# 3x3 stage, first two groups: the additions of an item's columns recorded in front of the next combinations

## The chip, the cores and the metric

The kernel runs on one core of one Trainium2 chip. Its time is the device time of that core in microseconds, the median of three runs. All arithmetic is in 32-bit floating point.

## The reference

Two residual bottleneck layers follow one another on an image tensor of 64 x 1024 x 14 x 14:

```
def layer(x, w1, b1, g1, be1, w2, b2, g2, be2, w3, b3, g3, be3, residual_scale):
    out = relu(bn(conv(x, w1, b1, stride=1, pad=0), g1, be1))     # 1x1, 1024 -> 256
    out = relu(bn(conv(out, w2, b2, stride=1, pad=1), g2, be2))   # 3x3,  256 -> 256
    out = bn(conv(out, w3, b3, stride=1, pad=0), g3, be3)         # 1x1,  256 -> 1024
    out = softplus(residual_scale)[0] * out
    return relu(x + out)
# bn: mean and variance over batch and pixels, per channel, of the batch itself
```

The case concerns the 3x3 convolution of both layers. Its input and output have 256 channels, held as two slots of 128 partitions.

## The kernel before, in words

Each layer is a 1x1 stage, then the 3x3 stage (`conv2`), then a 1x1 stage. The 256-channel image `y_all` stays on chip throughout. In the 3x3 stage it is worked on in place.

**Tiling.** The 64 images are cut into 8 groups of 8 images (`NG`, `GI`). The rows of a group are not convolved directly: combinations of rows are formed, each is multiplied by transformed filters, and the products are combined back into output rows. There are six such combinations per group (`NF`), taken in the pairs (1, 2), (3, 4), (5, 0). In this text they are **items**, numbered through a layer from 0 to 47. Items 0 to 5 belong to group 0, items 6 to 11 to group 1. Items of the pair (3, 4) have three tile rows, and their matmuls are 168 columns wide; the others have four and are 224 wide.

**Making an item's input.** `combine(g, pair)` records on VectorE (DVE) the work for both items of a pair. For the pair (3, 4) its first part is one large difference of rows into the scratch tile `steps` (L768), two combinations into `r` (L771 and L772, through the helper at L636), and `add_columns`, the additions into `sums` (L667). Its second part, recorded one step later, is `diffs` (L689) and `v` (L681). Each part ends with the loads of filters (`ua`, `ub`) for one item, issued on the SP queue. In what follows "the combinations of item 8" means the first part for the pair of items 8 and 9, and likewise "of item 14" for items 14 and 15.

**Multiplying.** TensorE (PE) takes, for each item in turn, four sets of eight matmuls: `l` of this item, the even `columns` of this item, `m` of the next item, and the odd `columns` of this item. `m` is copied by ScalarE (ACT) into the banks `columns` of the next item (L846, or L844 with a bias for the first item of a group) before that item's `columns` matmuls accumulate on it. There are **two** pairs of banks `columns`, so item i+2 gets the banks of item i. `l` is copied by ACT into `ls` (L866).

**Finishing.** `finish()` is a generator that takes one item per step. Each step begins with `add_to` (L885), which adds the banks `columns` and `ls` into a tile `f`: the additions of columns. This is the last reader of the item's banks. Further DVE work then combines the `f` tiles into output rows of `y`. For groups 0 and 1 the last step of a group, items 5 and 11, first records `middle_rows()` (four `stt` on DVE at L636, `y<-f,fb` and `y<-fc,fa`), then the `add_to`, then two accumulating DMAs on the POOL queue (L982). For later groups `middle_rows()` comes at an earlier step.

**Order.** A planner turns the recorded program into one instruction stream for each engine. Work recorded earlier has precedence, but an instruction that is not yet ready by the planner's reckoning is passed by a later one that is; instructions marked `keep_in_program_order` stay behind everything recorded before them on their engine. TensorE's matmuls are so marked. The DVE instructions that the change touches are not.

The loop over items records, for item k, its `l` copies, its even columns, the start of the next item, ACT's side work (`long_work`), its odd columns, `finished.send(item)`, and the part of the combinations for an item three places on. For k = 5 and k = 11 alone (`NF - 1`, `2 * NF - 1`) that last part is recorded ahead of `finished.send`.

Of the kernel before, what the change touches and what calls it, by code (L numbers as in the profile page):

```python
# [69 lines left out]
RT, NF = 4, 6  # L70
# [20 lines left out]
def bottlenecks(ctx: ExitStack, tc: tile.TileContext, x, w1s, w2s, w3s, pars, out):  # L91
# [85 lines left out]
    def busy(psum, tag, n, with_=None):  # L177

        v = ident if with_ is None else with_
        for i in range(n):  # L180
            matmul(psum.tile(448, tag), v, v[:, :1].to_broadcast([P, 448]), start=True, stop=True)
# [412 lines left out]
    def conv2(b, par, aff, early, rest):  # L594
# [434 lines left out]
        def items():  # L1029
            for g, pair in pairs[1:]:  # L1030
                yield from combine(g, pair)

        def long_work(g, k):

            i = ("norm 0", "norm 1", 0, 1, 2, 3)[k] if g else (None, "norm 0", "norm 1", None, None, None)[k]
            if g + 1 == NG:
                i = (0, 1, 2, 3, None, None)[k]
            if i in ("norm 0", "norm 1"):  # L1040
                s = int(i[-1])
                norm(s, y_grp[:, s, g + 1], aff, act)
            elif i is not None:
                o = i // 2
                moment(y_all[:, o, (g - 1) * GPX : g * GPX], idle, o, i % 2, g - 1)
# [13 lines left out]
        coming, finished = items(), finish()  # L1059
# [28 lines left out]
        queue = queue[1:] + list(itertools.islice(coming, 1))  # L1088
        for k in range(1, NG * NF):
            item, more = queue[0], queue[1:2]  # L1090
            qs = both_columns
            copy = act if k < 4 else nc.scalar.activation
            if k > 1:
                item.middle(copy=copy)
            if more:
                item.columns(qs[0])
                qs = qs[1:]
            for v in more:
                v.start(copy)
            if k == 1:  # L1100
                queue += list(itertools.islice(coming, 1))
            long_work(*divmod(k, NF))
            item.columns(*qs)
            if k in (NF - 1, 2 * NF - 1):
                queue += list(itertools.islice(coming, 1))
            finished.send(item)
            queue = queue[1:] + list(itertools.islice(coming, k not in (1, NF - 1, 2 * NF - 1)))
        busy(psum, "m", 7)

    def conv3(psum, t, o, w3, tag=None):  # L1110
# [405 lines left out]
    class Border:  # L1516
# [17 lines left out]
        def begin(self):  # L1534


            self.xpool.close()
            self.scope = ExitStack()
            early = self.scope.enter_context(
                tc.tile_pool(name=f"early_{self.b}", bufs=1, side="right", reuse_waits="tile")  # L1540
            )
            self.work = conv2(self.b, par[self.b], self.aff, early, self.rest)
# [193 lines left out]
```

## Time and profile before

| what | value |
|---|---|
| median of three runs | 1921.81 us (1921.47 to 1922.11) |
| the profiled execution | 1921.13 us, of which the span of the profile is 1919.3 us |
| granted TensorE clock | 1.0 |
| busy share of the span: PE, DVE, ACT, POOL | 99%, 80%, 57%, 30% |
| 3x3 stage of the first layer | about 304 to 584 us |
| 3x3 stage of the second layer | about 1258 to 1540 us |
| in 304 to 584 us: PE, DVE, ACT, POOL busy | 277.0, 269.3, 198.2, 45.6 us of 280 |

Starts are in microseconds from the beginning of the span. In the timelines each row is a run of like instructions: start, duration, engine, line, operation, output<-input, number, and in square brackets the idle time before it with what ended it. The recorded durations of neighbouring DVE instructions overlap by some 0.08 us, so the distance between starts is the time that one of them takes from its engine. In the list of stretches the columns are: stretch, its length, then the busy time and the number of instructions for PE, PEld (weight loads), DVE, ACT and POOL, the granted clock, the share of the DMA engines and GB/s. In the chain of waits each row is a piece of the chain that ended last: start, duration, engine, tile and line.

### The profile page before, as it was taken

To read this page: it belongs to the slowest core of one execution; us is meant where nothing else is said; L and a number is where in the kernel's file an instruction comes from. 1 tells how busy PE (TensorE), PEld (TensorE's weight loads), DVE (VectorE), ACT (ScalarE), POOL (GpSimd) and SP (SyncE) were. 2 spreads that over 40 slices of the span, in tenths; PEclk is the share of its full clock that TensorE was granted. 3 is DMA by queue.
4 is the path that set the end of the run, shared out by engine and by line. 5 is a ranking of instruction groups with operands and counts; after the bars stand their busy time and mean duration, and the time that the engine had idled before them with its cause. 6 is when DMAs were issued, how large, how long until landed. Compare 5 with 4: busy or idle time off the path is not lost.

```text
span 1919.3 us, 28730 instructions
## 1 busy us (share of the span) xinstructions
PE 1902.5 (99%) x10236; PEld 1596.2 (83%) x10236; DVE 1543.0 (80%) x2491; ACT 1087.0 (57%) x2160; POOL 571.7 (30%) x682
## 2 busy tenths in 40 slices
PE   9999999999999999999999999999999999999999
PEld 5555557999998799999999999989999986555555
DVE  5787767999998866676776767789999986888886
ACT  2222214677778255555555555556777682666666
POOL 0111100211204133433433333302121041666664
PEclk9999999999999999999999999999999999999999
DMA  7777644887856544444444444358878466899998
GB/s 291 272 249 273 220 153 156 206 212 211 214 170 172 193 159 169 169 168 181 177 180 168 168 168 176 124 179 210 211 209 222 142 172 243 292 324 346 329 338 303
DMA packets 198527, 408.77 MB, mean 213 GB/s; under 512 B 37104, under 2 KB 175024, under 8 KB 181872
## 3 DMA queue, kind: packets, MB, share of 16 engines
q1 hardware_dynamic: 159712, 321.85, 48.9%
q0 software_dynamic: 33056, 34.03, 8.6%
q10 hardware_dynamic: 5616, 51.06, 6.4%
q8 instruction: 81, 1.33, 0.3%
q14 instruction: 62, 0.51, 0.1%
HBM read 263.75 MB, written 115.34 MB: 198 GB/s over the span
## 4 chain that ended last, share of the span: by engine, by line
PE 93%; DVE 2%; ACT 2%; DMA 1%; POOL 1%; issue 1%; SPq 0%; DVEq 0%; ACTq 0%; POOLq 0%
PE ay L175 17%; PE cy L175 17%; PE columns L175 14%; PE cp L175 11%; PE ap L175 9%; PE m L175 7%; PE l L175 6%; PE cx L175 5%; PE ax L175 4%; PE ps L175 1%; ACT y L338 1%; DMA x<-mid 0%; DMA home<-y 0%; ACT home L338 0%; POOL home L1186 0%
## 5 line engine op out<-in xcount | busy, mean ns | idle before, releaser
L338 ACT ACTIVATE cu<-cy,scale 128x196 f32<-128x196 f32 (+1 forms) x552 | 256.8, 474 | 277.5 <-PE cy L175 272.3
L175 PE MATMUL columns<-v,ub 128*128 128x224 f32 (+1 forms) x1536 | 302.4, 338 | 4.8 <-ACT columns L846 3.9
L338 ACT ACTIVATE x<-x,shift 128x392 f32<-128x392 f32 x452 | 255.0, 613 | 73.1 <-POOL x L530 54.0
L175 PEld LDWEIGHTS columns<-v,ub 128*128 128x128 f32 x1536 | 268.8, 188 | 11.0 <-ACT columns L846 5.8
L504 DVE SCALAR_TENSOR_TENSOR x<-cp,scale,x 128x196 f32<-128x196 f32 (+1 forms) x368 | 178.0, 484 | 96.2 <-PE cp L175 94.9
L175 PE MATMUL cy<-ct,ws 128*128 128x196 f32 (+1 forms) x736 | 221.8, 383 | 1.2 <-ACT cu L338 1.2
L175 PE MATMUL ay<-at,ws 128*128 128x196 f32 (+1 forms) x768 | 212.7, 382 | 0.0
L525 POOL TENSOR_TENSOR x<-x,cu 128x196 f32<-128x196 f32 (+1 forms) x184 | 159.7, 868 | 171.7 <-ACT cu L338 163.9
L530 POOL TENSOR_TENSOR x<-x,cu 128x392 f32<-128x392 f32 x124 | 125.9, 1015 | 191.8 <-DVE x L504 191.8
L175 PEld LDWEIGHTS ay<-at,ws 128*128 128x128 f32 x768 | 139.3, 190 | 34.5
L175 PEld LDWEIGHTS cy<-ct,ws 128*128 128x128 f32 x736 | 133.4, 190 | 36.4 <-ACT cu L338 4.3
L175 PE MATMUL l<-diffs,ub 128*128 128x224 f32 (+1 forms) x768 | 149.6, 337 | 0.3 <-ACT sd L1478 0.3
L551 POOL TENSOR_TENSOR x<-x,cu 128x392 f32<-128x392 f32 x120 | 122.0, 1017 | 86.2 <-DVE x L504 67.8
L175 PE MATMUL m<-sums,ua 128*128 128x224 f32 (+1 forms) x752 | 146.0, 336 | 0.1
L338 ACT ACTIVATE au<-ay 128x196 f32<-128x196 f32 (+1 forms) x140 | 53.4, 382 | 149.6 <-PE ay L175 146.8
L175 PEld LDWEIGHTS l<-diffs,ub 128*128 128x128 f32 x768 | 134.6, 189 | 1.2 <-ACT sd L1478 0.6
L504 DVE SCALAR_TENSOR_TENSOR x<-cx,scale,x 128x196 f32<-128x196 f32 (+1 forms) x184 | 89.0, 484 | 56.7 <-PE cx L175 56.6
L175 PEld LDWEIGHTS m<-sums,ua 128*128 128x128 f32 x752 | 131.5, 189 | 1.3 <-DVE sums L667 0.7
L175 PE MATMUL cy<-y,w 128*128 128x196 f32 (+1 forms) x408 | 125.3, 393 | 0.0
L175 PE MATMUL cx<-y,w 128*128 128x196 f32 (+1 forms) x400 | 122.6, 391 | 0.0
L175 PE MATMUL cp<-y,ws 128*128 128x196 f32 (+1 forms) x368 | 113.6, 390 | 0.2 <-DVE x L504 0.2
L175 PE MATMUL cy<-ct,w 128*128 128x196 f32 (+1 forms) x368 | 111.0, 383 | 0.5 <-ACT cu L338 0.5
(238 smaller groups left out, 3913.6 us busy)
## 6 DMA issues: line engine op xcount, KB each, us to landing
x<-in_x SPq DMA_DIRECT2D x62, 1568.0 KB, 6.9
ub<-u SPq DMA_DIRECT2D x92, 768.0 KB, 5.2
x<-mid SPq DMA_DIRECT2D x32, 1568.0 KB, 8.2
mid<-x ACTq DMA_DIRECT2D x31, 1568.0 KB, 5.1
out<-x SPq DMA_DIRECT2D x123, 392.0 KB, 5.5
ua<-u SPq DMA_DIRECT2D x92, 256.0 KB, 3.1
u<-y POOLq DMA_DIRECT2D x48, 256.0 KB, 5.7
home<-y SPq DMA_DIRECT2D x70, 96.0 KB, 3.5
```

The costliest lines, as they stand in the source:

```text
L175: tc.keep_in_program_order(nc.tensor.matmul(*args, **kw))
L338: tc.keep_in_program_order(nc.scalar.activation(*args, **kw))
L504: nc.vector.scalar_tensor_tensor(v, bank, self.scale[:, o : o + 1], v, ALU.mult, ALU.add)
L525: nc.gpsimd.tensor_add(self.part(1, 1), self.part(1, 1), u3)
L530: nc.gpsimd.tensor_add(v, v, self.u12)
L551: nc.gpsimd.tensor_add(v, v, self.u12[:, i * self.n : (i + 1) * self.n])
```

## The change

For items 5 and 11 the special order is dropped. `finished.send(item)` is recorded first, and the combinations of the item three places on (8 and 14) after it, as for the other items. The same two places exist in both layers, so four places in the program change. No instruction is added or removed.

```
             long_work(*divmod(k, NF))
             item.columns(*qs)
-            if k in (NF - 1, 2 * NF - 1):
-                queue += list(itertools.islice(coming, 1))
             finished.send(item)
-            queue = queue[1:] + list(itertools.islice(coming, k not in (1, NF - 1, 2 * NF - 1)))
+            queue = queue[1:] + list(itertools.islice(coming, k > 1))
```

What is exchanged at each place: on DVE the four `stt` of `middle_rows()` and the `add_to` against L768, L771, L772 and L667; and the two DMAs of L982 on the POOL queue against two filter loads on the SP queue. ACT has no instruction in either part.

## The prediction

> **What bounds the kernel now.** I read the page first: busy shares, then the list of waits of the two 3x3 stages, then stretches of 10 us around items 5 to 14, then the chain of waits and the timelines there.
>
> ```profile
> PE 1902.5 (99%) x10236; PEld 1596.2 (83%) x10236; DVE 1543.0 (80%) x2491; ACT 1087.0 (57%) x2160; POOL 571.7 (30%) x682
> ```
>
> TensorE sets the time. A change that adds no instruction can gain only where PE waits. In the 3x3 stage of layer 0, PE is idle about 3 us, and these stretches hold most of what lies behind item 5:
>
> ```profile
> 340.00:350.00 10.00, 10.00 (x54) 9.88 (x53) 10.00 (x12) 3.87 (x10) 3.88 (x3) 1.00 0.98 227
> 350.00:360.00 10.00, 8.92 (x54) 8.49 (x53) 8.02 (x10) 8.28 (x18) 2.56 (x2) 1.00 0.88 197
> 360.00:370.00 10.00, 10.00 (x64) 9.96 (x63) 9.89 (x11) 8.88 (x19) 0.00 (x0) 1.00 0.70 229
> 380.00:390.00 10.00, 9.45 (x52) 9.02 (x51) 9.90 (x13) 6.35 (x13) 2.57 (x2) 1.00 0.83 218
> ```
>
> PE loses 1.08 us in 350 to 360 (item 7, two behind item 5) and 0.55 us in 380 to 390 (item 13, two behind item 11). Layer 1 shows the same: 8.64 us busy of 10 in 1304 to 1314, and 9.45 in 1334 to 1344. The chain of waits names the cause of the first:
>
> ```profile
> 350.17 0.42 DVE y L636
> 350.59 1.01 DVE f L885
> 351.68 0.54 ACT columns L846
> 352.24 0.54 ACT columns L846
> 352.82 1.81 PE columns L175 x8
> ```
>
> PE's `columns` of item 7 need ACT's copy of `m` into their banks; those are item 5's banks, and their last reader, the `add_to` of item 5, runs only at 350.5. The DVE timeline shows why it is so late:
>
> ```profile
> 341.99 1.75 DVE L681 TENSOR_TENSOR v<-r 128x1536 f32<-128x1536 f32 x1
> 343.66 2.95 DVE L768 TENSOR_TENSOR steps<-y 128x2688 f32<-128x2688 f32 x1
> 346.53 0.50 DVE L636 SCALAR_TENSOR_TENSOR y<-f,fb 128x336 f32<-128x336 f32 x1
> 346.95 1.62 DVE L636 SCALAR_TENSOR_TENSOR r<-steps 128x672 f32<-128x672 f32 x2
> 348.49 0.50 DVE L636 SCALAR_TENSOR_TENSOR y<-fc,fa 128x336 f32<-128x336 f32 x1
> 348.90 0.85 DVE L667 TENSOR_TENSOR sums<-r 128x672 f32<-128x672 f32 x1
> 349.67 0.50 DVE L636 SCALAR_TENSOR_TENSOR y<-f,fb 128x336 f32<-128x336 f32 x1
> 350.09 0.50 DVE L636 SCALAR_TENSOR_TENSOR y<-fc,fa 128x336 f32<-128x336 f32 x1
> 350.51 2.08 DVE L885 TENSOR_TENSOR f<-columns,ls 128x896 f32<-128x896 f32 x2
> 357.43 1.09 DVE L885 TENSOR_TENSOR f<-columns,ls 128x896 f32<-128x896 f32 x1 [1.84 <-PE columns L175]
> ```
>
> DVE has no gap from 341.99 to 350.51. The odd columns of item 5 ended on PE at 344.12 (start 342.43, duration 1.69), so the `add_to` stood ready for over 6 us behind the combinations of item 8. The `y` row between L768 and the two `r` shows a middle row slipping in while the `r` were not ready: the middle rows were ready by then.
>
> **The change, step by step.** Four places, each with the same exchange on DVE. By distance between starts, a middle row takes 0.42 us (346.53 to 346.95), so four take 1.68; the `add_to` of 896 columns 1.00; L768 2.87; the two `r` 1.54; `sums` 0.77.
>
> *What the new order gives behind item 5, layer 0.* From 343.66: middle rows to 345.34, `add_to` of item 5 to 346.34, L768 to 349.21, the `r` to 350.75, `sums` ready at 350.75 + 0.85 = 351.60. If L768 passes the `add_to`, the `add_to` ends at 343.66 + 1.68 + 2.87 + 1.08 = 349.29; `sums` is the same.
>
> *The wait that goes.* `m` of item 7 ends at 348.69 on PE, so ACT's two copies (1.09 us, and ACT is idle for 2.45 us before them) can run to about 349.8, or to 350.4 behind an `add_to` that ended at 349.29. Undisturbed, `columns` start 1.51 us after `l` (343.96 to 345.47): 350.07 + 1.51 = 351.58 instead of 352.82. That is 1.24 us. The set after the wait also takes 1.66 us to its successor instead of 1.54, 0.12 more. Item 7 gives 1.36.
>
> *The other three, in the same way.* Item 13, layer 0: `l` at 385.03, `columns` at 387.26 instead of 386.54, plus 0.10: 0.82. Layer 1, item 7: `l` at 1304.12, `columns` at 1307.16 instead of 1305.63, plus 0.11: 1.64. Item 13: `l` at 1339.36, `columns` at 1341.59 instead of 1340.87, plus 0.10: 0.82. Sum: 1.36 + 0.82 + 1.64 + 0.82 = 4.64 us.
>
> *What is late next.* `m` of item 8 needs `sums`. Without the stall it starts at 351.58 + 1.54 = 353.12, with `sums` ready at 351.60: 1.5 us to spare. Behind item 11, DVE takes up L768 at 378.09: middle rows, `add_to`, L768, `r`, `sums` end 378.09 + 1.68 + 1.00 + 2.87 + 1.54 + 0.85 = 386.03, against `m` of item 14 at 388.89 - 0.82 = 388.07: 2.0 to spare. If the `add_to` of item 6 (1.00, ready at 350.3) slips in ahead of `sums`, the reserve at item 8 falls to 0.5; price nothing. Then `diffs` (0.76) ends by about 353.5, and `l` of item 8 wants it at 353.12 + 1.14 + 1.54 = 355.80; `v` ends by 354.8, wanted at 356.9. The following `add_to` of item 7 sat 1.84 us idle for PE in the trace, and moves up with PE. So no new wait of PE, and the 1.2 us of earlier matmuls behind item 7 are taken from idle DVE time: 1.84 us there and 1.16 us at 391.18 behind item 13, more than the gain of each place.
>
> *The queues.* POOL's two accumulating DMAs of item 5 (L982, 2.56 us on POOL, 5.2 us to landing) start some 2 to 5 us earlier, right behind those of L965, which leave POOL at 344.42. They have POOL's queue to themselves then, and nothing of PE's waits for their landing. The two filter loads on SP are issued when their buffers come free (348.72 and 350.26, as PE is done with earlier items), not by the order of recording: nothing. More DMA at once around 347 meets `ub` loads with a share of 0.98 already; their median landing is 5.2 us, while the load issued at 344.15 is wanted by item 8's `l` at 355.8, so a doubled landing is still hidden.
>
> [...] When the `add_to` of item 7 waited 1.84 us for PE, nothing else ran on DVE. [...] Here it is reached at 345.34, 1.2 us after PE's end at 344.12; behind item 11 at 379.77, 0.7 us after PE's end at 379.11. [...]
>
> *Sum.* The profiled execution took 1921.13 us (span 1919.3 and 1.83 around it), 0.68 under the median. 1921.13 - 4.64 = 1916.5 in its terms, 1917.2 in those of the median. Bounds: without the slow first sets (0.43 in all) 1917.6; with the `add_to` slipping behind the two `r` as well (end 350.83, copies to 351.95, 0.37 late at item 7) about 1918. On the far side, the small wait for L846 between 435 and 470 (0.18) may go too, and with DVE's reserve a little more: 1915.8.
>
> **The rivals.**
>
> *Only part of the gain.* The planner's clock differs from the chip's, and later instructions that are not pinned may change places after the shift: f, fa, fb of items 7 to 14 on DVE, the copies on ACT. Half of the gain lost is 2.3 us: 1919.5. For it: in group 2, where the additions are recorded first already, L768 starts at 413.51 and the `add_to` follows at 416.38. Against it: that stretch has no stall.
>
> *The change does nothing.* If the planner holds the middle rows or the banks for unready, L768 to `sums` go first as now: 1921.8. Against it stands the middle row at 346.53.
>
> *Slower: the sums come last.* DVE is busy 34.3 of 35 us a group, so there is little room to catch up. If DVE takes the `add_to` of item 6 in front of L768 too, it stands until that item's odd columns end at 350.24: 351.3, then L768 to 354.2, the `r` to 355.7, `sums` 356.55. `m` of item 8 would start at 356.6 instead of 354.48, 2.1 us late against the trace. Item 14, by the same sum: 385.2, 386.2, 389.1, 390.6, 391.4 against 388.89, 2.5 late. Layer 1: 1304.3, 1305.3, 1308.2, 1309.7, 1310.5 against 1308.81, 1.7, and 2.5 again. Sum 8.8 us: 1930.6. It decides from where `sums` of item 8 is ready later than 354.4. Against it: DVE would have to stand idle for 4 us before ready work, and in the trace its waits of over 1 us have nothing ready behind them.
>
> **How the numbers follow.** Forecast, all four waits gone: 0.60, at 1917.2, of its own 1915.8 to 1918.3. Part of the gain: 0.14, 1918 to 1921. No change: 0.08. Slower: 0.18, from just above 1922 to 1930.6. A measurement of this kernel tells a difference from none at about 0.2%, 3.84 us, so the line lies at 1917.97. Over it: the forecast, and 0.02 of the partial case: 0.62. Within: 0.12 + 0.08 = 0.20. Slower by over 0.2%: 0.18. The range 1915.8 to 1923.0 leaves out most of the slower case and little below.
>
> **What would show it.** Right: the `add_to` of item 5 at 345 to 349 us, ACT's L846 for item 7 waiting for PE `m` and not for `f`, PE busy 10.00 of 10 in 350 to 360 and 380 to 390 and in their places in layer 1, `m` of item 8 at about 353.1, the end of the 3x3 stage 2.2 us earlier in layer 0 and 4.6 in layer 1. Wrong: PE waiting for DVE `sums` L667 at items 8 or 14, idle DVE in front of an `add_to` at 346, or the gain of 4.6 us given back behind 400 us by other orders on DVE or ACT.

## The result and the profile after

The changed kernel takes 1918.22 us (median; 1917.24 to 1921.93), the kernel before 1921.81 (1920.76 to 1923.22) on the same chips: a ratio of 0.9982 with a 95% interval of 0.9975 to 0.9989. That is 3.6 us less where 4.6 were forecast, 0.19%, and the interval reaches over both sides of the 0.2% line. The profiled execution took 1919.69 us, 1.47 over the median, and has to be read with that.

The page's first part, PE, PEld, DVE, ACT and POOL, is almost unchanged; the instructions are the same:

```profile
PE 1901.9 (99%) x10236; PEld 1595.2 (83%) x10236; DVE 1543.6 (80%) x2491; ACT 1086.2 (57%) x2160; POOL 572.0 (30%) x682
```

The stretches of 10 us that were shown of the kernel before (stretch, length, then busy time and number for PE, PEld, DVE, ACT, POOL, then clock, DMA share, GB/s):

```profile
340.00:350.00 10.00, 10.00 (x54) 9.88 (x53) 9.97 (x12) 4.47 (x11) 6.43 (x5) 1.00 1.04 234
350.00:360.00 10.00, 10.00 (x63) 9.91 (x62) 9.16 (x11) 8.75 (x20) 0.00 (x0) 1.00 0.97 239
360.00:370.00 10.00, 9.84 (x60) 9.54 (x58) 9.90 (x11) 8.23 (x18) 0.00 (x0) 1.00 0.66 198
380.00:390.00 10.00, 10.00 (x56) 9.90 (x55) 9.56 (x10) 6.68 (x16) 2.57 (x2) 1.00 1.06 235
```

The idle 1.08 and 0.55 us of PE are gone. But 360 to 370, full before, now lacks 0.16. The DVE timeline behind item 5 (start, duration, instruction):

```profile
343.84 0.50 DVE L636 SCALAR_TENSOR_TENSOR y<-f,fb 128x336 f32<-128x336 f32 x1
...
345.09 0.50 DVE L636 SCALAR_TENSOR_TENSOR y<-fc,fa 128x336 f32<-128x336 f32 x1
345.51 1.09 DVE L885 TENSOR_TENSOR f<-columns,ls 128x896 f32<-128x896 f32 x1
346.51 2.95 DVE L768 TENSOR_TENSOR steps<-y 128x2688 f32<-128x2688 f32 x1
349.50 1.63 DVE L636 SCALAR_TENSOR_TENSOR r<-steps 128x672 f32<-128x672 f32 x2
351.16 0.86 DVE L667 TENSOR_TENSOR sums<-r 128x672 f32<-128x672 f32 x1
```

The `add_to` of item 5 moved from 350.51 to 345.51, and `sums` from 348.90 to 351.16. ACT's copy into the banks of item 7 now waits for `m` itself, and PE's `columns` start at 351.76 without a gap:

```profile
348.91 1.09 ACT L846 ACTIVATE columns<-m 128x448 f32<-128x448 f32 x2 [2.08 <-PE m L175]
```

**Where the rest went.** PE runs the same 10236 matmuls in the same order in both kernels, so the n-th start can be set against the n-th. The difference changes only where a wait comes or goes. The steps of the first start behind each wait, in us against the profile of the kernel before (minus is earlier; the columns E1 to E7 belong to the experiments below):

| place | changed | again (E5) | E1 | E2 | E3 | E4 | E7 |
|---|---|---|---|---|---|---|---|
| layer 0, item 7 | -1.24 | -1.24 | -1.24 | 0 | -1.24 | +0.32 | -1.24 |
| item 9 | +0.33 | +0.32 | +0.33 | 0 | +0.15 | 0 | 0 |
| item 13 | -0.71 | -0.72 | 0 | -0.71 | -0.71 | +0.32 | -0.71 |
| item 15 | +0.28 | +0.28 | 0 | 0 | 0 | 0 | 0 |
| items 18 to 24 | +0.60 | +0.59 | +0.47 | 0 | +0.59 | 0 | +0.19, +0.37 |
| item 27 | -0.35 | -0.35 | -0.35 | +0.31 | -0.35 | 0 | -0.35 |
| layer 1, item 7 | -1.52 | -1.52 | -1.52 | 0 | -1.52 | +0.32 | -1.52 |
| item 13 | -0.71 | -0.72 | 0 | -0.71 | -0.72 | +0.32 | -0.71 |
| item 27 | +0.29 | +0.27 | 0 | +0.28 | -0.27 | 0 | -0.35 |
| both 3x3 stages, whole | -2.97 | -3.27 | -2.42 | -0.90 | -3.98 | +1.38 | -4.35 |
| between the two stages | -0.97 | -0.45 | -0.31 | -0.92 | -0.58 | -0.77 | -1.00 |
| median less that of before, same rounds | -3.59 | -2.99 | -2.25 | -0.11 | -4.34 | +1.14 | -4.52 |

The row "whole" is what the difference grew by from ahead of item 7 to late in each stage. It is more than the steps, since the eight matmuls behind a wait mostly take some 0.10 us longer, and that comes or goes with the wait: with it the four waits give 1.34, 0.81, 1.62 and 0.81 us, 4.58 in all against the 4.64 forecast. It holds 0.25 late in layer 1 too, where a weight load of PE came late in this profile alone. What came about between the stages can't be put down to the change: it is waits of PE near 602 and 644 us in the profile of the kernel before, and E4, which gains nothing in the 3x3 stages, has 0.77 there as well.

The four waits went as the prediction had them. New, small ones came at items 9, 15 and 21, and at item 27 one went in layer 0 and one came in layer 1. The chain of waits at item 9 (start, duration, what):

```profile
360.65 0.28 ACT y L939
360.93 0.28 ACT y L946
361.21 0.35 ACT columns L846
...
361.58 0.44 ACT columns L846
...
362.06 0.99 PE columns L175 x5
```

The banks were free, and `m` was done. ACT was not: it went through a row copy from `fa` (L939) and one from `fb` (L946) first. In the kernel before, these two stood there as well: ACT came to the copies of `m` at 360.98 there and at 361.11 here. At item 15 it was 395.61 and 395.08. So ACT's copies of `m` moved up by nothing and by 0.53 us, while PE had moved up by 1.2 and 1.5. At item 21 the order on ACT is another: one row copy even stands between the two halves of the copy of `m`, and itself waits for DVE:

```profile
427.61 0.43 ACT L846 ACTIVATE columns<-m 128x336 f32<-128x336 f32 x1 [0.40 <-PE m L175]
429.53 0.39 ACT L939 ACTIVATE y<-fa 128x224 f32<-128x224 f32 x1 [1.49 <-DVE fa L917]
429.82 0.43 ACT L846 ACTIVATE columns<-m 128x336 f32<-128x336 f32 x1
```

### The profile page after: what moved, and what is told of

Same layout as the page of the kernel before. It is cut to its first block, busy times and chain, and to the rows that moved or that the text cites. A ratio compares the mean times of both kernels' runs of the same rounds, so it can differ in the third digit from the quotient of the medians.

```text
span 1917.9 us, 28732 instructions
## 1 busy us (share of the span) xinstructions
PE 1901.9 (99%) x10236; PEld 1595.2 (83%) x10236; DVE 1543.6 (80%) x2491; ACT 1086.2 (57%) x2160; POOL 572.0 (30%) x682
## 4 chain that ended last, share of the span: by engine, by line
PE 92%; DMA 2%; DVE 2%; ACT 2%; POOL 1%; issue 1%; SPq 0%; DVEq 0%; ACTq 0%; POOLq 0%
PE ay L175 17%; PE cy L175 17%; PE columns L175 14%; PE cp L175 11%; PE ap L175 10%; PE m L175 7%; PE l L175 6%; PE cx L175 5%; PE ax L175 4%; PE ps L175 1%; DMA x<-mid 1%; ACT y L338 1%; ACT home L338 1%; DMA home<-y 1%; POOL home L1184 0%
```

## The experiments

Theory A: PE waited for the banks of items 5 and 11, which their late `add_to` held. Rival B: the gain is that of the other order as such. Theory A2: what was given back is ACT, held in order behind L939 and L946.

**E1, item 5 alone.** The old order stays behind item 11 (in E1 and E2 the same condition changes in the line of `queue` too):

```
-            if k in (NF - 1, 2 * NF - 1):
+            if k == 2 * NF - 1:
```

> New order behind item 5 alone (both layers), item 11 keeps the old one. Theory A (the gain is PE's wait for the banks of items 5 and 11, which their add_to frees late): PE's waits before the columns of item 7 go (1.36 us in layer 0, 1.64 in layer 1), those of item 13 stay (0.55 us idle each): 3.0 us less, some 0.3 to 0.6 given back by small new waits for L846 in the same group: 1919.2 us. Rival B (the gain comes from the planner's other order of DVE and ACT through the whole stage, not from the two waits): no tie to item 5; either all of the gain of the full change, 1918.2, or none, 1921.8, and waits that move elsewhere.

Measured: 1919.43 us, ratio 0.9986 (0.9977 to 0.9995). The steps of item 7 are there, those of item 13 are zero. 2.25 us less, where A had 2.5.

**E2, item 11 alone.**

```
-            if k in (NF - 1, 2 * NF - 1):
+            if k == NF - 1:
```

> New order behind item 11 alone. Theory A: PE's waits before the columns of item 13 go (0.82 us in each layer), those of item 7 stay (1.08 and 1.36 us idle): 1.64 us less, some 0.3 to 0.6 given back: 1920.4 us. Rival B: as above, 1918.2 or 1921.8.

Measured: 1921.57 us, ratio 1.0000 (0.9991 to 1.0009). The steps at item 13 are those of A. At the end of both 3x3 stages PE is 1.82 us ahead, but 0.92 of that came between them; the stages themselves give 0.90 where A had 1.0 to 1.3, and the median shows nothing of it. In this profile the last 1x1 stage loses more than that again, 1.60 us of it at one place, where a load `x<-mid` lands late. The local half of the forecast held, the total did not (see E5).

**E3, the `add_to` alone**, with its two DMAs. The middle rows stay behind the combinations. Against the kernel before:

```
-                if g < 2:
-                    middle_rows()
                 if by_transfer:
                     f = outputs(cb)
                     ...
+                    if g < 2:
+                        yield
+                        middle_rows()
                     continue
```
```
             item.columns(*qs)
+            finished.send(item)
             if k in (NF - 1, 2 * NF - 1):
                 queue += list(itertools.islice(coming, 1))
-            finished.send(item)
+                next(finished)
```

> Only the add_to of items 5 and 11 with its two DMAs goes in front of the combinations; the middle rows stay behind them. Theory A: all four waits go as in the full change, since the add_to then starts at about 346.5 in layer 0 (behind L768): 4.64 us less what small new waits on ACT take: 1917.5 to 1918.5 us. Rival B: the middle rows' place matters too, half of the gain or less: 1920 us or more.

Measured: 1917.34 us, ratio 0.9975 (0.9965 to 0.9985): somewhat more than the whole change gives (in the 3x3 stages 3.98 us against 2.97 and 3.27). Its DVE timeline:

```profile
343.35 2.95 DVE L768 TENSOR_TENSOR steps<-y 128x2688 f32<-128x2688 f32 x1
346.22 1.09 DVE L885 TENSOR_TENSOR f<-columns,ls 128x896 f32<-128x896 f32 x1
```

The `add_to` behind L768 is early enough, and the middle rows' place gives nothing.

**E4, the middle rows alone.** The `add_to` is held behind `sums`, and ACT's order is that of before. The loop is that of E3:

```
                 if g < 2:
                     middle_rows()
+                    yield
                 ...
-                    f = outputs(cb)
+                    f = new("f", cb.lines // GI)
+                    ins = nc.vector.tensor_add(halves(f), cb.by_columns(cb.banks), cb.by_columns(cb.ls))
+                    if g < 2:
+                        tc.keep_in_program_order(ins)
```

> The other half alone: the middle rows go in front of the combinations, and the add_to of items 5 and 11 is held behind them (behind sums), as late as before; ACT's order is that of the kernel before. Theory A: the add_to runs at about 350.5 in layer 0 as before, and the four waits stay: 1921.8 us. Rival B: the middle rows moved, so a good part of the gain comes: 1919 to 1920 us.

Measured: 1922.82 us, ratio 1.0005 (0.9996 to 1.0014). The chain there, where L982 is the line of the `add_to` in this kernel:

```profile
351.62 1.09 DVE f L982
...
352.80 0.54 ACT columns L846
...
353.36 0.54 ACT columns L846
...
353.94 1.81 PE columns L175 x8
```

All four waits stayed, and each grew by 0.32 us: the profile's earlier stages lie 0.79 later here, and the `add_to` 1.11 later (351.62 against 350.51). PE follows the `add_to` to the hundredth. With E3 this settles that the `add_to`, and not the middle rows, carries the gain.

**E5, the changed kernel again.**

> The changed kernel once more, for a second profile. In its first profile 1.4 and 0.4 us were lost near 1793 and 1813 us, where PE waited for VectorE's x and that for a load x<-mid. If these are chance landings of single loads, the second profile lies nearer the median, 1918.2 us, with the 3x3 stages ahead by the same 2.05 and some 2 us; if they belong to the new order's earlier start of the last stage, they come again at the same places.

Measured: 1918.37 us, ratio 0.9986 (0.9977 to 0.9995), profiled execution 1918.07. The list of PE's waits from 1560 to 1900 us (engine, line, what it waited for: us, times, longest) is this:

```profile
PE cp L175 <- DVE zt L1221: 0.7, 1, 0.7
PE cy L175 <- ACT cu L338: 0.5, 1, 0.5
PE cp L175 <- DVE x L504: 0.2, 1, 0.2
```

The 3x3 stages repeat to 0.02 us in each step. The 1.4 and 0.4 us near 1793 and 1813 did not come again, so the new order does not bring them of itself. The loss of 1.60 us in E2's profile is at the place of the 1.4; no other profile has more than 0.5 there. That E2's median lost more than its neighbours is not explained by this and stays open.

**E6, three pairs of banks, old order.** `l` and `m` get one bank each, and the first `l2` borrows one of the third pair:

```
-            return psum.pool.tile([P, 2, 512], FP, tag="columns", name="columns", bufs=2)
+            return psum.pool.tile([P, 2, 512], FP, tag="columns", name="columns", bufs=3)
-            border.go_on(Psum(scope, ["l"], l=2, m=2), pool, stats2)
+            border.go_on(Psum(scope, ["l"], l=1, m=1), pool, stats2)
```

> The kernel before with its old order, but three pairs of banks columns instead of two (l and m with one bank each instead of two). Item 7 then doesn't take item 5's banks. Theory A: the four waits go although the add_to of items 5 and 11 stays at 350.5 and in its place behind the combinations: 4.64 us less, about 1917 to 1918 us, if single l and m banks cost nothing. Rival B (the order of VectorE's work itself): no gain, 1921.7.

Measured: 1919.69 us, ratio 0.9992 (0.9983 to 1.0001). This kernel leaves out the first matmul that starts one bank of the third pair before it is accumulated on, so its sums are wrong; it serves for the times alone. The four waits went (-1.24, -0.72, -1.52, -0.72). Against that the seven closing identity matmuls of the stage (14 records), which all go to the one bank of `m`, took 7.38 us instead of 5.45 in layer 0.

**E7, ACT's copies pinned.** The changed kernel, with two lines replaced; `act` is the kernel's helper that issues the same copy and keeps it in program order:

```
-                        nc.scalar.activation(out_rows[0][:, :, full], a[:, :, full], AF.Copy)
+                        act(out_rows[0][:, :, full], a[:, :, full], AF.Copy)
-                        nc.scalar.activation(end, d[:, :, full], AF.Copy)
+                        act(end, d[:, :, full], AF.Copy)
```

> The changed kernel with ACT's two row copies L939 and L946 kept in program order, so that they no longer stand in front of the copies of m (L846) while they wait for fa and fb; VectorE's order is unchanged. Theory A2 (the small new waits of PE, 0.33 at 362, 0.28 at 396 and 0.6 at 430 us and alike in layer 1, come from ACT being held in order behind L939 and L946): they go, 1.0 to 1.5 us less than the changed kernel: 1917.0 us. Rival: they come from the add_to of the item two before being late on VectorE: nothing changes, 1918.2.

Measured: 1916.84 us, ratio 0.9978 (0.9969 to 0.9987). DVE's instructions stand in the same order as in the changed kernel; ACT and PE behind item 7:

```profile
359.76 0.59 ACT L757 ACTIVATE steps<-y 128x448 f32<-128x448 f32 x1
360.23 0.93 ACT L846 ACTIVATE columns<-m 128x336 f32<-128x336 f32 x2
361.07 1.60 ACT L338 ACTIVATE idle<-y,center 128x1568 bf16<-128x1568 f32 x1
```
```profile
360.29 1.30 PE L175 MATMUL l<-diffs,ub 128*128 128x168 f32 x8
361.42 1.32 PE L175 MATMUL columns<-v,ub 128*128 128x168 f32 x8
```

Set against the changed kernel, PE gains 0.33 at item 9, 0.28 at item 15, 0.60 at item 21 and 0.63 at item 27 of layer 1, and loses 0.19 and 0.37 at items 19 and 24. A2 holds at the four places: with it the 3x3 stages give 4.35 us.

**E8, E3 and E7 together.**

> The add_to alone in front of the combinations, with ACT's copies L939 and L946 kept in program order. Theories A and A2 together: the four waits and most of the small ones are gone, 1916.7 us or a little less; if the pinned copies cost as much elsewhere, 1917.3.

Measured: 1917.41 us, ratio 0.9982 (0.9973 to 0.9991): a miss of the lower figure. The wait at item 18 remains and is larger (+0.83 against the kernel before, +0.59 in E3). It is not one of A2: ACT stands idle for 3.90 us there, until DVE's `add_to` (L885) frees the banks. By the medians the pinned copies are worth nothing on top of E3; in the profiles the two 3x3 stages give 4.30 us against 3.98.

**E9, the rival in which `sums` come last.** L768 is issued twice for items 8 and 14:

```
-                run(nc.vector.tensor_sub(d, y[:, :, 2 * LINE :], y[:, :, : (H - 2) * LINE]))
+                for _ in range(2 if g in (1, 2) else 1):
+                    run(nc.vector.tensor_sub(d, y[:, :, 2 * LINE :], y[:, :, : (H - 2) * LINE]))
```

> The changed kernel with the difference L768 of items 8 and 14 issued twice (the second one writes the same values again), which puts 2.87 us more of VectorE's work in front of sums. This prices the rival in which the sums come last. In the changed kernel sums of item 8 are ready at 352.02, 1.29 us before m of item 8 starts at 353.31; sums of item 14 at 385.39, 1.96 us before 387.35. Theory: PE waits for L667 at item 8 by some 1.6 us, or 2.6 if the next add_to slips in as well, and at item 14 by 0.9 to 1.9, in both layers alike: 5 to 9 us more, 1923 to 1927 us. Rival: VectorE has room elsewhere in the group and nothing is seen, 1918.2.

Measured: 1933.72 us, ratio 1.0058 (1.0043 to 1.0074), 15.5 us more than the changed kernel, far over the expected 5 to 9. The waits lie at the upper end of what was worked out (the PE timeline, behind items 7 and 13):

```profile
352.07 1.70 PE L175 MATMUL columns<-v,ub 128*128 128x224 f32 x8
356.24 1.41 PE L175 MATMUL m<-sums,ua 128*128 128x168 f32 x8 [2.47 <-DVE sums L667]
...
391.99 2.02 PE L175 MATMUL m<-sums,ua 128*128 128x168 f32 x8 [1.88 <-DVE sums L667]
393.80 2.80 PE L175 MATMUL columns<-v,ub 128*128 128x224 f32 x8
```

The starts against the changed kernel step by 2.63 and 2.04 in layer 0, 2.58 and 2.04 in layer 1: 9.3 us. But the eight `columns` behind the second wait took 2.80 us instead of 1.69: the clock. In the stretches around the four waits (third figure: PE's busy time; eighth: granted clock):

```profile
352.00:354.00 2.00, 1.77 (x10) 1.38 (x8) 2.00 (x3) 1.71 (x6) 0.00 (x0) 1.00 1.27 220
354.00:356.20 2.20, 0.00 (x0) 0.00 (x0) 2.17 (x4) 0.63 (x2) 0.00 (x0) 1.00 0.84 302
356.20:358.00 1.80, 1.76 (x11) 1.75 (x12) 1.80 (x2) 0.31 (x1) 0.00 (x0) 1.00 0.05 20
390.10:392.00 1.90, 0.02 (x2) 0.01 (x1) 1.87 (x4) 0.63 (x2) 0.00 (x0) 1.00 0.92 315
392.00:393.00 1.00, 1.00 (x6) 1.00 (x7) 1.00 (x2) 0.00 (x0) 0.00 (x0) 0.82 0.17 57
393.00:394.00 1.00, 1.00 (x5) 1.00 (x5) 0.97 (x1) 0.00 (x0) 0.00 (x0) 0.50 0.07 25
394.00:396.40 2.40, 2.40 (x9) 2.18 (x8) 0.86 (x1) 2.33 (x3) 0.00 (x0) 0.57 0.35 104
396.40:398.00 1.60, 1.60 (x13) 1.60 (x12) 1.33 (x2) 1.60 (x6) 0.00 (x0) 1.00 0.08 18
1312.00:1314.00 2.00, 0.13 (x1) 0.13 (x2) 1.97 (x4) 0.63 (x2) 0.00 (x0) 1.00 0.83 298
1314.00:1316.00 2.00, 2.00 (x9) 2.00 (x10) 1.90 (x3) 0.00 (x0) 0.00 (x0) 0.56 0.04 13
1316.00:1318.00 2.00, 2.00 (x8) 1.83 (x8) 0.81 (x1) 1.77 (x3) 0.00 (x0) 0.59 0.19 54
1318.00:1320.00 2.00, 2.00 (x15) 1.99 (x14) 1.45 (x2) 2.00 (x6) 0.00 (x0) 1.00 0.29 85
1350.00:1352.00 2.00, 0.73 (x4) 0.73 (x5) 1.97 (x4) 0.63 (x2) 0.00 (x0) 0.95 0.43 160
1352.00:1354.00 2.00, 2.00 (x9) 1.92 (x8) 1.90 (x2) 0.51 (x2) 0.00 (x0) 0.50 0.01 4
1354.00:1356.00 2.00, 2.00 (x9) 1.88 (x8) 0.30 (x2) 2.00 (x3) 0.00 (x0) 0.70 0.45 129
1356.00:1358.00 2.00, 2.00 (x16) 2.00 (x15) 1.97 (x2) 1.94 (x6) 0.00 (x0) 1.00 0.08 19
```

Behind three of the four waits the clock was below 1.00 for a while. Worked out from the rows, as length times the clock that is missing, it took 1.71 us of PE's time behind the second wait (0.18 of 1.00 us, 0.50 of 1.00, 0.43 of 2.40), and 1.70 behind each of the two in layer 1. With these 5.1 us, waits and clock make some 14.4 us of the 15.5.

**E10, three pairs of banks, started, old order.** The third pair is written by matmuls before it is accumulated on, and the closing matmuls alternate (the two lines of E6's edit belong to it too):

```
+        third = columns()[:, :, : MS * second.n].rearrange("p q (o n) -> p q o n", o=MS)
-        l, m, l2 = first.bank("l"), second.bank("m"), second.bank("l")
+        l, m, l2 = first.bank("l"), second.bank("m"), third[:, EVEN]
+        n = MS * second.n
+        matmul(third[:, ODD].rearrange("p o n -> p (o n)"), ident, ident[:, :1].to_broadcast([P, n]), start=True, stop=True)
...
-        busy(psum, "m", 7)
+        for i in range(7):
+            busy(psum, "ml"[i % 2], 1)
```

> The kernel before in its old order with three pairs of banks columns, now with both banks of the third pair written by a first matmul before they are accumulated on, and the seven closing identity matmuls of the stage alternating between the banks of m and l, so that they don't wait for one another. Theory A: the four waits go with the add_to as late as before, and the 2.3 us that the closing matmuls lost in layer 0 with a single bank (0.22 us at each step) do not come again: 1917 to 1918 us, with some 0.5 us for the filling. Rival B: 1921.5.

Measured: 1916.29 us, ratio 0.9970 (0.9959 to 0.9982). The `add_to` of item 5 is as late as ever, and nothing waits for it; DVE and PE:

```profile
350.46 2.08 DVE L885 TENSOR_TENSOR f<-columns,ls 128x896 f32<-128x896 f32 x2
```
```profile
350.05 1.67 PE L175 MATMUL l<-diffs,ub 128*128 128x224 f32 x8
351.56 1.71 PE L175 MATMUL columns<-v,ub 128*128 128x224 f32 x8
```

That is theory A without any change of DVE's order at this place. Part of this kernel's 5.8 us (the median of before in the same rounds is 1922.13) comes from the stage's start and its closing matmuls, not from the waits.

**E11 and E12, the same with pinned copies, old and new order.** E10 with the edit of E7; E12 has the change too.

> Old order, three pairs of banks filled at the start, and ACT's copies L939 and L946 in program order. In the run with three pairs alone PE still waited 0.13, 0.34 and 0.60 us at places where the changed kernel waits behind those copies. Theory A2: these go, 1916.3 less 0.7 to 1.1: 1915.4 us. Rival: with a third pair the copies of m have time enough, nothing changes: 1916.3.

> The same with the new order. Theory A: with three pairs of banks the add_to of items 5 and 11 frees nothing that PE waits for, so the order behind items 5 and 11 is worth nothing more: the same as with the old order, 1915.4 us, within 0.5. Rival B (the new order is worth something by itself): 1 us or more apart.

Measured: E11 1914.69 us, ratio 0.9967 (0.9954 to 0.9979), the fastest of all; E12 1915.44 us, ratio 0.9968 (0.9956 to 0.9981). Against E10, E11 loses none and gains 0.13, 0.35 and 0.60 at just the three places named. Between E12 and E11 lie 0.75 us, a little over what was expected. In the profiles E12 has two more waits of 0.19 and 0.18 (items 19 of both layers). With three pairs of banks the new order gains nothing.

## Why the prediction was right, and what it missed

The forecast was 1917.2, faster, within 1915.8 to 1923.0; measured 1918.22. That lies at the upper edge of the forecast's own stretch, 1915.8 to 1918.3, and in that of the partial rival, 1918 to 1921. It is nearer than the working deserves: of the 4.64 us the 3x3 stages kept 2.97 in the first profile and 3.27 in the second, 1.07 and 1.10 of it by the end of layer 0, where 2.2 was named. Step by step:

- **The wait that goes.** The four gains were set at 1.24, 0.72, 1.53 and 0.72 us without the slow first sets; the starts stepped by 1.24, 0.71, 1.52 and 0.71. The cause named, two pairs of banks and a late `add_to`, is shown by E3, E4 and E10.
- **The new order on DVE.** The `add_to` was expected at 345.34 and came at 345.51, with PE 0.18 later from the start. In layer 0 nothing slipped between. Behind item 11 L768 did pass the `add_to`, a case that was allowed for.
- **What is late next, on DVE.** `sums` of item 8 were to be 1.5 us ahead of `m`, those of item 14 2.0; measured 1.29 and 1.96. In layer 1 the `add_to` of item 6 did slip in: `sums` were done at 1304.87, 0.45 ahead of `m` at 1305.32, where 0.5 was worked out.
- **The step that failed** is its last sentence, "So no new wait of PE". Only DVE's products were followed to their users. ACT's copies of `m` for items 9, 15 and 21 were not, and by PE's earlier start those became late: 0.33, 0.28 and 0.60 us in layer 0, 0.29 at item 27 in layer 1, against 0.35 won at item 27 in layer 0 (the small wait that the far side of the range allowed for). This is the partial rival in kind, on "the copies on ACT", and its price of 2.3 us was too large. Its mechanism, that instructions change places, fits item 21; at items 9 and 15 the row copies stood in front before the change too, and only PE moved. E7 shows the cause. An instruction that is not ready and holds what stands behind it was looked for on DVE, where it cost nothing: the `add_to` of items 5 and 11 started at 345.51 and 381.88 in layer 0 with no idle time before them. On ACT, where it was not looked for, the row copies in front of the copies of `m` cost some 1.5 us (0.33, 0.28, 0.60 and 0.29).
- **The slower rival** did not come about, and it was priced by its waits alone, 8.8 us. E9, which delays `sums` by other means, shows that waits of that length, 1.9 to 2.5 us, cost 9.3 us, and another 5.1 us in clock.
- **The last stage.** A gain in front of it was carried over whole to the end; a late load took 1.4 us in one execution of the changed kernel and none in another. The chances treated the line at 0.2% as if the forecast stood clear of it, with 0.60 on a time 0.8 us below the line; the measured 0.19% lies on the line.

## What to carry to other kernels

When a wait is for a buffer, look for the last reader of the buffer's previous owner, and either move that reader forward alone or add a buffer: the rest of what was recorded with it need not move. When the bounding engine moves forward, check every operand of it again, on each engine's queue and not only on the one that was changed: a short copy that waits can hold an urgent one behind it on an engine that is idle, as at item 21, where ACT stood idle for 1.49 us in front of a row copy and only then made the second half of the copy of `m`. In E9 three of four PE waits of 1.88 to 2.47 us were followed by a loss of 1.7 us in clock, so removing such a wait can be worth more than its length.

## What the runs showed of the hardware

After PE waits of 1.88 us (twice) and 2.42 us in E9 the granted clock fell, to a mean of 0.50, 0.50 and 0.56 in the lowest of the rows shown, and eight matmuls of 224 columns took 2.53 to 2.80 us instead of 1.70. After one of 2.47 us it stayed at 1.00, and so it did after the waits of 1.08 and 0.55 us in the kernel before. So the length of the wait alone does not tell the three from the fourth; what does is not shown.

In E6 seven identity matmuls of 448 columns (14 records) that follow one another into one bank took 7.38 us, and in the kernel before, into two banks in turn, 5.45: with one bank the weight loads in E6's trace waited for the matmul before them (six waits, 4.7 us in all).
